# A state-space mixer on one core: half of the convolved tiles transposed by VectorE and through memory instead of TensorE

## The chip, the cores and the metric

The kernel runs on one core of a Trainium2 chip. The metric is device time in microseconds (us), the median of several runs.

## The reference

Two gated layers over `x` of shape (2, 512, 512), all in float32. Layer 0 normalizes, mixes by autocorrelation and gates by a small feed-forward block. Layer 1 normalizes, runs a Mamba-like mixer and gates by a second feed-forward block. The change lies in the mixer. Cut to what matters:

```python
proj = einsum('bsd,od->bso', h, in_proj_w)             # 512 -> 8192 gate | 8192 hid + 1024 B + 1024 C | 128 dt
hBC  = silu(causal_conv(hBC, conv_w, conv_b))          # 4 taps along the sequence
hid  = hBC[..., :8192].reshape(b, s, 128, 64)          # 128 heads of 64
hc   = (hid * dt[..., None]) in chunks of 128 steps
M    = einsum('bcihn,bcjhn->bcijh', C, B) * L          # L: decays inside a chunk
Y_diag = einsum('bcijh,bcjhp->bcihp', M, hc)
states = einsum('bclhn,bhcl,bclhp->bchpn', B, decay_states, hc)
Y_off  = einsum('bclhn,bchpn,bhcl->bclhp', C, prev_states, exp(A_cs))
y   = Y_diag + Y_off + Dp * hid
out = einsum('bsd,od->bso', rmsnorm_by_group(y * silu(gate)), out_proj_w)
```

B and C are shared by groups of 16 heads; there are 8 groups.

## The kernel before

**Tiles.** One *tile* `s` holds 128 channels (two heads) of one batch row, channels on the partitions and the 512 sequence positions (4 chunks of 128) along the free dimension. A *unit* is one group and one batch row: 8 tiles. There are 16 units and 128 tiles. A *step* `d` (63 of them, then `tail()`) treats two tiles in each of four stages at once: it finishes products for the tiles `a` = 2d, 2d+1, prepares the next pair `n` = 2d+2, 2d+3, projects and convolves the pair after that, `h` = 2d+4, 2d+5, and squares the previous pair `p`. `t` is the place of the pair in its unit: 0, 2, 4 or 6, so a unit takes four steps.

**A tile's way.** `Values` projects a pair of tiles on TensorE (seven block products instead of eight) into PSUM (`pjh`). `first_tap` and `taps` convolve (ScalarE, then three VectorE instructions), `silu()` applies SiLU on ScalarE to all that was convolved since it was last called; the result is `hid[s]`, channels on partitions. For the products the sequence positions must lie on partitions: in the next step `transposed(s)` makes four 128x128 TensorE transposes into the PSUM tile `px`, and `values(s, px)` multiplies them on VectorE by per-position, per-head factors from `sls` into `hc` (4 chunks) and `hcd` (3 chunks). `clamp` and `decays` make the decay matrices in `css[s]` (`cs`; the exponential on ScalarE, the product with `CB` on VectorE). `begun` multiplies `hcd` with the transposed B (`Bss`) on TensorE into `pn`; `states` copies chunk 0 into `st` (ScalarE) and runs the recurrence over chunks in four VectorE instructions. `starts` multiplies the loaded `eb` by C on GpSimd (POOL). In the step after, `products(s)` multiplies `hc` with the decays and `st` with `eb` into `py`, and `finish_y` scales and adds `Dp * hid` on VectorE. `Gates` projects the gate like `Values`; `Output` (`o`) does the output projection of the previous unit, spread over its steps, adding into `acc` on VectorE (L1553) and using block sums that `o.sums(0)` and `o.sums(1)` make on POOL. `pair_sums` makes the sums `sh` and `sw` of the weights on POOL. `inner` projects and convolves B and C of the next unit at t=0 (`BT`, `CT`), and `inner_products` transposes B and multiplies B and C at t=4.

**Order.** The whole part is under a manual schedule: every engine runs its instructions in the order in which the code issues them. All loads go through one queue, SP (`nc.sync`): `load_sums` (`cs`, three buffers), `load_starts` (`eb`, two), `load_rest` (`el`), `load_gate`, `load_hid` (weights `wg`, `wh`), `load_bc`, `load_out` (`wo`, once per group, 2 MB) and `load_slice`. At a step's beginning SP waits in `load_sums` for TensorE's first products, which free a `cs` buffer. The wk pool's tag `sq` has two buffers, `hid` four, `st`, `hc`, `hcd` two each. PSUM tag `tr` has one buffer, `pj` three, `yy` two, `of` and `de` one each.

57 of the 63 steps have the interleaved order (`if gates:`); steps 0 to 3, 60 and 62 have the plain one (`else:`), in which the second tile's `px` lies in a `pj` bank. Step 0 is the first of unit 0, and `head()` prepares tiles 0 to 3.

Of the kernel before, what the change touches and what calls it, by code (L numbers as in the profile page):

```python
# [15 lines left out]
P = 128  # L16
D = 512
B = 2
S = 512
# [29 lines left out]
def fused_kernel(  # L49
# [1000 lines left out]
    with ExitStack() as sm:  # L1050
# [148 lines left out]
        def finish_y(s, py):  # L1199
# [7 lines left out]
                y, hid.pop(s), Dcol[:, ct : ct + 1], y, ALU.mult, ALU.add  # L1207
            )

        def square(s):  # L1210

            u, t = divmod(s, GT)
            if t == 0:
                sums[u] = wk.tile([P, S], F32, tag="sums", name=f"sums{u}", bufs=1)
                q = sums[u]
            else:
                q = wk.tile([P, S], F32, tag="sq", name=f"sq{s}", bufs=2)
            nc.scalar.activation(q, y_of(s), AF.Square)  # L1218

            def add():  # L1220
                if t > 0:
                    nc.gpsimd.tensor_tensor(sums[u], sums[u], q, ALU.add)  # L1222

            return add
# [5 lines left out]
                nc.tensor.transpose(px[:, c, :], hid[s][:, bass.ts(c, P)], ident)  # L1230
            return px

        def values(s, px):

            u, g, b, t, h0 = place(s)
            pxh = px.rearrange("p c (h d) -> p c h d", h=2)
            hc = wk.tile([P, NCH, P], F32, tag="hc", name=f"hc{s}")
            hcd = wk.tile([P, NCH - 1, P], F32, tag="hcd", name=f"hcd{s}")
            for dst, j, n in ((hc, 0, NCH), (hcd, 1, NCH - 1)):
                nc.vector.tensor_tensor(  # L1240
                    dst.rearrange("p c (h d) -> p c h d", h=2),
                    pxh[:, 0:n],
                    pair(sls[g][:, j, b * NCH : b * NCH + n, h0 : h0 + 2]),
                    ALU.mult,
                )
            hcs[s] = hc
            return hcd
# [31 lines left out]
            return pn  # L1279

        def states(s, pn):

            u, g, b, t, h0 = place(s)
            st = wk.tile([P, NCH - 1, P], F32, tag="st", name=f"st{s}")
            nc.scalar.copy(st[:, 0, :], pn[:, 0, :])  # L1285
            for c in range(1, NCH - 1):
                for hh in range(2):
                    cols = bass.ts(hh, HP)
                    nc.vector.scalar_tensor_tensor(  # L1289
                        st[:, c, cols],  # L1290
                        st[:, c - 1, cols],
                        sls[g][:, 2, b * NCH + c, h0 + hh : h0 + hh + 1],
                        pn[:, c, cols],
                        ALU.mult,
                        ALU.add,
                    )
            sts[s] = st

        def starts(s):

# [68 lines left out]
        class Gates:  # L1369
# [65 lines left out]

        def inner_products(u):

            pb = psum.tile([P, NCH, P], F32, tag="tr", name=f"pb{u}", bufs=1)
            for c in range(NCH):
                nc.tensor.transpose(pb[:, c, :], BTs[u][:, bass.ts(c, P)], ident)  # L1440
# [9 lines left out]
            Bss[u] = wk.tile([P, NCH, NST], F32, tag="Bs", name=f"Bs{u}", bufs=1)  # L1450
# [143 lines left out]
        def head():  # L1594
# [40 lines left out]
            conv(*first)  # L1635
            conv(*channels(3))
            silu()
            nc.scalar.activation(*held, AF.Silu)

        def plain(d):  # L1640
# [4 lines left out]
        def step(d):  # L1645
# [16 lines left out]
                load_slice(h[0] // (B * GT))  # L1662
            for s in n[1:]:
                load_sums(s)
            if b == 1 and t == 0 and 0 < g < NG:
                load_out(g)
            for s in h[:1]:
                load_sums(s)
            for s in n:
                load_starts(s)  # L1670
            if n:
                load_gate(n[0] // 2)
            if h and h[0] // 2 < tiles // 2 - 1:
                whs[h[0] // 2 + 1] = load_hid(h[0] // 2 + 1)
            if b == 0 and t == 2 and 0 <= g < NG - 1:
                wbc[g + 1] = load_bc(g + 1)
            if d == steps - 2:
# [32 lines left out]
            hids = made_ahead.pop(d, None)  # L1710
            if not gates:
                first = [channels(s) for s in h[:1]]
                pxs = [transposed(s, s % 2) for s in n]

            def root():
                if t == 2 and went:
# [27 lines left out]
            if gates:  # L1744

                def output(n=1):
                    if o:
                        o.multiply(n)
# [5 lines left out]
                late = t == 2  # L1754
                px = transposed(n[0])
                hids.multiply(1, 5)
                hcd = [values(n[0], px)]
                decays(n[0], 0)
                hids.copy(0, 0)
                hids.multiply(2, 3)  # L1760
                hids.add(0, 0)
# [2 lines left out]
                output()  # L1764
                if projected is not None:
                    b_of = inner(projected, 0)
                px = transposed(n[1])
                hids.multiply(6)
                if not late:
                    added()  # L1770
                hcd.append(values(n[1], px))
                decays(n[1], 0)
                if projected is not None:
                    conv(*b_of)
                hids.copy(0, 1)
                gates.multiply(1, 5)
                decays(n[1], 1)
                starts(n[1])
                if t == 4 and o:
                    o.sums(1)  # L1780
# [50 lines left out]
                taps(*hids.sum(1))  # L1831
                output()
                added()
                states(n[1], pn)
                if projected is not None:
                    first_tap(*c_of)
                pss = squares()
                gates.multiply(3)
                silu()
                gates.add(0, 1)  # L1840
                output(int(t < 6))
                gates.silu()
                mean(pss)
# [4 lines left out]
            else:  # L1848
# [9 lines left out]
                    starts(s)  # L1858
                for f in [square(s) for s in p]:
                    f()  # L1860
                hcd = [values(s, px) for s, px in zip(n, pxs)]
                root()
                if projected is not None:
                    conv(*inner(projected, 0))
# [189 lines left out]
```

## Time and profile before

| What | Value |
|---|---|
| Time, median of 3 runs | 2217.05 us (2216.99 to 2217.43) |
| Span of the profiled execution | 2213.2 us; its own time is not listed beside it |
| TensorE (PE) busy | 2191.3 us, 99% |
| VectorE (DVE) busy | 1513.8 us, 68% |
| ScalarE (ACT) busy | 1299.4 us, 59% |
| GpSimd (POOL) busy | 1321.7 us, 60% |
| DMA engines | 146 GB/s on average |
| A unit of four interleaved steps | 104 us (208.0 us for two) |

The part under the manual schedule's `head()` and steps takes the span from about 530 us on. A line such as `L1240` is a line of the kernel printed above. A transposed second tile stands as the second `px` group of a step (L1230). "PEld" is TensorE's weight load, which overlaps its matmuls. In the timeline a TensorE group's duration contains the pipeline's tail, so groups overlap a little; the chain of waits gives the net time of each group.

### The profile page before, as it was taken

To read this page: it belongs to the slowest core of one execution; us is meant where nothing else is said; L and a number is where in the kernel's file an instruction comes from. 1 tells how busy PE (TensorE), PEld (TensorE's weight loads), DVE (VectorE), ACT (ScalarE), POOL (GpSimd) and SP (SyncE) were. 2 spreads that over 40 slices of the span, in tenths; PEclk is the share of its full clock that TensorE was granted. 3 is DMA by queue.
4 is the path that set the end of the run, shared out by engine and by line. 5 is a ranking of instruction groups with operands and counts; after the bars stand their busy time and mean duration, and the time that the engine had idled before them with its cause. 6 is when DMAs were issued, how large, how long until landed. Compare 5 with 4: busy or idle time off the path is not lost.

```text
span 2213.2 us, 35453 instructions
## 1 busy us (share of the span) xinstructions
PE 2191.3 (99%) x12460; PEld 1712.6 (77%) x12460; DVE 1513.8 (68%) x2985; ACT 1299.4 (59%) x2864; POOL 1321.7 (60%) x1234
## 2 busy tenths in 40 slices
PE   8999999999999999999999999999999999999999
PEld 4545567765568888888888888888888888888877
DVE  5263577545777777777777677777777677777763
ACT  4131323214777667676767676767767676767671
POOL 4151523323457567776766686759576866766577
PEclk9999999999999999999999999999999999999999
DMA  4012266755544446444545454454446444544452
GB/s 174 1 58 75 80 226 221 255 195 195 176 143 129 148 140 190 133 135 124 167 133 148 152 175 128 134 162 129 134 141 187 138 145 124 167 124 133 141 187 97
DMA packets 195953, 323.51 MB, mean 146 GB/s; under 512 B 17728, under 2 KB 129984, under 8 KB 193344
## 3 DMA queue, kind: packets, MB, share of 16 engines
q1 hardware_dynamic: 189376, 300.28, 44.5%
q0 software_dynamic: 6400, 20.98, 2.5%
q8 instruction: 99, 1.62, 0.3%
q14 instruction: 78, 0.64, 0.1%
HBM read 294.45 MB, written 26.74 MB: 145 GB/s over the span
## 4 chain that ended last, share of the span: by engine, by line
PE 95%; DVE 2%; ACT 1%; DMA 1%; POOL 0%; issue 0%; SPq 0%; ACTq 0%; DVEq 0%
PE pjh L607 15%; PE of L1530 15%; PE gt L607 13%; PE py L1177 5%; PE pjbc L1139 5%; PE pf L1018 4%; PE pn L1276 4%; PE py L1186 4%; PE px L1230 3%; PE ofy L1530 2%; PE hu L361 2%; PE sh L522 2%; PE pg L607 2%; PE pu L607 2%; PE gty L607 2%; PE gt L1139 2%
## 5 line engine op out<-in xcount | busy, mean ns | idle before, releaser
L1301 POOL TENSOR_TENSOR eb<-CT,eb 128x768 f32<-128x768 f32 x128 | 230.0, 1818 | 342.9 <-DMA eb<-ea_d 287.1
L1254 ACT ACTIVATE cs<-cs,sl 128x128 f32<-128x128 f32 x1024 | 325.0, 390 | 0.6 <-DMA cs<-cs_d 0.6
L1158 DVE SCALAR_TENSOR_TENSOR hid<-pjh,cw,hid 128x511 f32<-128x511 f32 (+2 forms) x384 | 286.5, 746 | 43.1 <-ACT hid L1149 35.6
L1269 DVE TENSOR_TENSOR cs<-de,CB 128x512 f32<-128x512 f32 x256 | 175.4, 685 | 80.0 <-ACT de L1268 79.0
L1688 POOL TENSOR_TENSOR y<-y,sgt 128x512 f32<-128x512 f32 x124 | 176.1, 1440 | 11.6 <-ACT sgt L1410 9.7
L1177 PE MATMUL py<-cs,hc 128*64 128x128 f32 x2048 | 180.3, 276 | 0.0
L1222 POOL TENSOR_TENSOR sums<-sums,sq 128x512 f32<-128x512 f32 x110 | 140.1, 1273 | 61.3 <-ACT sq L1218 57.6
L1268 ACT ACTIVATE de<-cs 128x512 f32<-128x512 f32 x256 | 154.0, 602 | 28.9 <-DVE cs L1269 22.6
L1186 PE MATMUL py<-eb,st 128*64 128x128 f32 x1536 | 149.1, 273 | 0.0
L1289 DVE SCALAR_TENSOR_TENSOR st<-st,sl,pn 128x64 f32<-128x64 f32 x512 | 108.4, 275 | 59.4 <-ACT st L1285 59.4
L1553 DVE SCALAR_TENSOR_TENSOR acc<-of,rg,acc 128x256 f32<-128x256 f32 x188 | 90.2, 480 | 74.7 <-PE of L1530 74.4
L1354 ACT COPY hid<-pjh 128x256 f32<-128x256 f32 x171 | 63.6, 372 | 129.5 <-PE pjh L607 127.7
L1206 DVE SCALAR_TENSOR_TENSOR y<-hid,Dcol,y 128x512 f32<-128x512 f32 x128 | 133.8, 1045 | 4.5
L1177 PEld LDWEIGHTS py<-cs,hc 128*64 128x64 f32 x2048 | 121.5, 137 | 19.9 <-issue 18.1
L1205 DVE TENSOR_TENSOR y<-py,el 128x512 f32<-128x512 f32 x128 | 87.7, 685 | 57.1 <-PE py L1186 56.3
L1285 ACT COPY st<-pn 128x128 f32<-128x128 f32 x128 | 33.1, 264 | 153.3 <-PE pn L1276 153.3
L1530 PE MATMUL of<-wt,y 128*128 128x256 f32 x512 | 121.8, 381 | 0.0
L1139 PE MATMUL pjbc<-hT,wbc 128*128 128x512 f32 x256 | 117.4, 593 | 2.1 <-DVE BT L1158 1.3
L1530 PE MATMUL of<-wo,s 128*128 128x256 f32 x496 | 118.8, 382 | 0.0
L1276 PEld LDWEIGHTS pn<-hcd,Bs 128*128 128x128 f32 x768 | 104.7, 191 | 16.5 <-issue 11.3
L607 PE MATMUL pjh<-th,sh 128*128 128x256 f32 x456 | 117.3, 380 | 0.2 <-POOL sh L581 0.2
L607 PE MATMUL pjh<-hT,wh 128*128 128x256 f32 x456 | 117.2, 379 | 0.0
(356 smaller groups left out, 5518.7 us busy)
## 6 DMA issues: line engine op xcount, KB each, us to landing
cs<-cs_d SPq DMA_DIRECT2D x128, 512.0 KB, 4.3
eb<-ea_d SPq DMA_DIRECT2D x256, 192.0 KB, 6.0
wh<-in_in_wT SPq DMA_DIRECT2D x64, 512.0 KB, 9.2
wg<-in_in_wT SPq DMA_DIRECT2D x64, 512.0 KB, 7.4
el<-ea_d SPq DMA_DIRECT2D x256, 128.0 KB, 7.5
wo<-wo_d SPq DMA_DIRECT2D x16, 1024.0 KB, 8.4
wop<-in_out_wT SPq DMA_DIRECT2D x39, 256.0 KB, 2.8
wo_d<-wop POOLq DMA_DIRECT2D x39, 256.0 KB, 2.8
```

Of the source, the lines that this page charges most:

```text
L607: nc.tensor.matmul(ps, x[:, k, :], y[:, k, :], start=(first and k == 0), stop=(k == 1), skip_group_check=True,)
L1139: nc.tensor.matmul(ps, w_of(k), hT[:, k, bass.ts(b, S)], start=(k == 0), stop=(k == KD - 1))
L1158: nc.vector.scalar_tensor_tensor(dst[:, j:], ps[:, : S - j], cw[:, ct, KCONV - 1 - j : KCONV - j], dst[:, j:], ALU.mult, ALU.add,)
L1177: nc.tensor.matmul(py[bass.ts(hh, HP), bass.ts(c, P)], hc[:, c, bass.ts(hh, HP)], M[:, hh, bass.ts(c, P)], start=True, stop=(c == 0),)
L1186: nc.tensor.matmul(py[bass.ts(hh, HP), bass.ts(c, P)], st[:, c - 1, bass.ts(hh, HP)], cte[:, hh, bass.ts(c - 1, P)], start=False, stop=True,)
L1254: nc.scalar.activation(m[:, bass.ts(c, P)], m[:, bass.ts(c, P)], AF.Relu, bias=sls[g][:, 3, b * NCH + c, h0 + hh : h0 + hh + 1], scale=-1.0,)
L1268: nc.scalar.activation(pe, m, AF.Exp, scale=-1.0)
L1269: nc.vector.tensor_tensor(m, pe, CBs[s // GT].rearrange("p c i -> p (c i)"), ALU.mult)
L1276: nc.tensor.matmul(pn[:, c, :], Bss[s // GT][:, c, :], hcd[:, c, :], start=True, stop=True)
L1301: nc.gpsimd.tensor_tensor(eb_t[s], CTs[s // GT][:, P:].unsqueeze(1).to_broadcast([P, 2, S - P]), eb_t[s], ALU.mult,)
L1530: nc.tensor.matmul(ps, x[:, k, :], y[:, k, :], start=(first and k == 0), stop=(k == 3), skip_group_check=True,)
L1688: nc.gpsimd.tensor_tensor(y_of(s), y_of(s), sgs.pop(s), ALU.mult)
```

## The change

Of each pair of tiles only the first is still transposed by TensorE. The second is taken by a new function `turn(s)`, called behind `silu()` in the step that convolves it (and in `head()` for tile 3): one VectorE transpose, which turns 32x32 blocks, into a tile `to` of tag `sq`, and four DMAs on SP that write it to a scratch tensor in memory so that rows become sequence positions, in runs of 128 elements. `fetch(s)`, at the next step's beginning on SP, reads it back (256 KB) into `to`. `values(s)` without `px` then reads it from SBUF in four instructions instead of two from PSUM.

In the interleaved steps the order moves too: the first tile's first decay comes before its values; the second tile's values come behind its second decay; `states` of the second tile is split, so that ScalarE's copy stays where it was and the four VectorE instructions come behind the turn and `gates.add(0, 1)`. In `step`'s loads, `fetch` stands behind the first `load_sums`, `load_starts` moves behind the two weight loads, and `load_out` moves to the end. In the plain steps the second tile's values follow the first's. Last, `inner_products` transposes three chunks of B instead of four (the fourth was never read), and `Bss` holds three.

```diff
+        raw, sent = {}, {}
+
+        def turn(s):
+            to = wk.tile([P, S], F32, tag="sq", name=f"tn{s}", bufs=2)
+            nc.vector.transpose(
+                to.rearrange("p (q c e) -> p q c e", q=4, c=NCH),
+                hid[s].rearrange("p (c q e) -> p q c e", c=NCH, q=4),
+            )
+            dst = dram.tile([P, 4, P], F32, tag="tn_d", name=f"tn_d{s}", bufs=3)
+            for a in range(4):
+                nc.sync.dma_start(
+                    dst[:, a, :].rearrange("(q r) e -> r q e", q=4),
+                    to[32 * a : 32 * a + 32].rearrange("r (q e) -> r q e", q=4),
+                )
+            sent[s] = to, dst
+
+        def fetch(s):
+            to, src = sent.pop(s)
+            nc.sync.dma_start(to, src.rearrange("p a e -> p (a e)"))
+            raw[s] = to.rearrange("p (a c e) -> p a c e", a=4, c=NCH)
...
-        def values(s, px):
+        def values(s, px=None):
...
             for dst, j, n in ((hc, 0, NCH), (hcd, 1, NCH - 1)):
+                if px is None:
+                    dst = dst.rearrange("p c (a e) -> p a c e", a=4)
+                    for h in range(2):
+                        two = slice(2 * h, 2 * h + 2)
+                        f = sls[g][:, j, b * NCH : b * NCH + n, h0 + h]
+                        f = f.unsqueeze(1).unsqueeze(3).to_broadcast([P, 2, n, 32])
+                        nc.vector.tensor_tensor(dst[:, two], raw[s][:, two, 0:n], f, ALU.mult)
+                    continue
...
         def states(s, pn):
+            first_state(s, pn)
+            rest_of_states(s, pn)
...
-            pb = psum.tile([P, NCH, P], F32, tag="tr", name=f"pb{u}", bufs=1)
-            for c in range(NCH):
+            pb = psum.tile([P, NCH - 1, P], F32, tag="tr", name=f"pb{u}", bufs=1)
+            for c in range(NCH - 1):
...
             silu()
+            turn(3)
...
             for s in n[1:]:
                 load_sums(s)
-            if b == 1 and t == 0 and 0 < g < NG:
-                load_out(g)
+                fetch(s)
             for s in h[:1]:
                 load_sums(s)
-            for s in n:
-                load_starts(s)
             if n:
                 load_gate(n[0] // 2)
             if h and h[0] // 2 < tiles // 2 - 1:
                 whs[h[0] // 2 + 1] = load_hid(h[0] // 2 + 1)
+            for s in n:
+                load_starts(s)
+            if b == 1 and t == 0 and 0 < g < NG:
+                load_out(g)
...
-                pxs = [transposed(s, s % 2) for s in n]
+                pxs = [transposed(s) for s in n[:1]]
...
+                decays(n[0], 0)
                 hcd = [values(n[0], px)]
-                decays(n[0], 0)
...
-                px = transposed(n[1])
                 hids.multiply(6)
...
-                hcd.append(values(n[1], px))
                 decays(n[1], 0)
...
                 decays(n[1], 1)
+                hcd.append(values(n[1]))
                 starts(n[1])
...
-                states(n[1], pn)
+                first_state(n[1], pn)
...
                 silu()
+                for s in h[1:]:
+                    turn(s)
                 gates.add(0, 1)
+                rest_of_states(n[1], pn)
...
-                hcd = [values(s, px) for s, px in zip(n, pxs)]
+                hcd = [values(*x) for x in zip(n, pxs)]
+                hcd += [values(s) for s in n[1:]]
...
                 silu()
+                for s in h[1:]:
+                    turn(s)
```

More of the change, by code (lines that the diff above doesn't have):

```diff
@@ L1231, in transposed @@
             return px
-        def values(s, px):
+        def values(s, px=None):
             u, g, b, t, h0 = place(s)
-            pxh = px.rearrange("p c (h d) -> p c h d", h=2)
+            if px is not None:
+                pxh = px.rearrange("p c (h d) -> p c h d", h=2)
             hc = wk.tile([P, NCH, P], F32, tag="hc", name=f"hc{s}")
@@ L1281, in states, with first_state, rest_of_states @@
         def states(s, pn):
+            first_state(s, pn)
+            rest_of_states(s, pn)
+        def first_state(s, pn):
+            sts[s] = wk.tile([P, NCH - 1, P], F32, tag="st", name=f"st{s}")
+            nc.scalar.copy(sts[s][:, 0, :], pn[:, 0, :])
+        def rest_of_states(s, pn):
             u, g, b, t, h0 = place(s)
-            st = wk.tile([P, NCH - 1, P], F32, tag="st", name=f"st{s}")
-            nc.scalar.copy(st[:, 0, :], pn[:, 0, :])
+            st = sts[s]
             for c in range(1, NCH - 1):
@@ L1296, in states @@
                     )
-            sts[s] = st
         def starts(s):
@@ L1449, in inner_products @@
                 )
-            Bss[u] = wk.tile([P, NCH, NST], F32, tag="Bs", name=f"Bs{u}", bufs=1)
+            Bss[u] = wk.tile([P, NCH - 1, NST], F32, tag="Bs", name=f"Bs{u}", bufs=1)
             nc.scalar.copy(Bss[u], pb)
```

## The prediction

> **What bounds the kernel now.** I read the page first: busy time and the chain that ended last.
>
> ```profile
> PE 2191.3 (99%) x12460; PEld 1712.6 (77%) x12460; DVE 1513.8 (68%) x2985; ACT 1299.4 (59%) x2864; POOL 1321.7 (60%) x1234
> PE 95%; DVE 2%; ACT 1%; DMA 1%; POOL 0%; issue 0%; SPq 0%; ACTq 0%; DVEq 0%
> ```
>
> TensorE is the bound: 95% of the chain runs over it. The waits between 640 and 2100 us hold no PE wait at all, and of PE's weight loads only `PEld of L1530 <- DVE acc L1553`, 14 times at most 0.3 us: once per unit VectorE is just late there. So time falls only by what leaves PE, less any new PE wait. The chain's order shows the price of what leaves (start, us, what):
>
> ```profile
> 1340.36 0.44 PE pb L1440 x4
> 1344.89 0.59 PE px L1230 x4
> 1350.67 0.44 PE px L1230 x4
> ```
>
> The third row is the second tile's transposes, wedged between other products: 0.435 us, 0.109 each. A unit (four steps) takes 104 us. Next, the border between a unit's first step (t=0) and its second (t=2), because VectorE and ScalarE are densest there (start, us, engine, line, form):
>
> ```profile
> 1388.23 0.83 PE L1276 MATMUL pn<-hcd,Bs 128*128 128x128 f32 x6
> 1393.85 0.39 PE L1177 MATMUL py<-cs,hc 128*64 128x128 f32 x4
> 1394.07 0.39 PE L1186 MATMUL py<-eb,st 128*64 128x128 f32 x4
> 1389.10 0.27 ACT L1285 COPY st<-pn 128x128 f32<-128x128 f32 x1 [2.01 <-PE pn L1276]
> 1389.26 0.78 ACT L1149 ACTIVATE CT<-pjbc,cb,cw 128x512 f32<-128x512 f32 x1
> 1390.06 1.28 ACT L1591 ACT_TABLE_LOAD   x1
> 1391.36 0.63 ACT L1591 ACTIVATE BT<-BT 128x512 f32<-128x512 f32 x1
> 1391.89 1.14 ACT L1591 ACTIVATE hid<-hid 128x512 f32<-128x512 f32 x2
> 1390.34 0.85 DVE L1289 SCALAR_TENSOR_TENSOR st<-st,sl,pn 128x64 f32<-128x64 f32 x4
> ```
>
> Before, the four `st` updates ran at 1390.34, during ScalarE's silus, 2.9 us before PE read the second state (1394.07). ScalarE's last silu ended at 1393.03.
>
> **Removed.** Steps 0 to 62 each lose four transposes, and 16 units one B transpose. Step 0 waits for VectorE anyway (PE idle 1.12 us before `pn` at 570.93), so 62 x 0.435 + 16 x 0.109 = 27.0 + 1.7 = **28.7 us** leave PE. The Bs copy shrinks from 0.59 us by a quarter on ScalarE, off the path.
>
> **VectorE, `values`.** Two instructions reading PSUM (0.683 and 0.547, pitches 0.60 and 0.46) become four reading SBUF. The 256-element row of L891, both inputs in SBUF, has 416 ns at least; with pitch about 0.33 for 256 and an estimated 0.265 for 192 elements, four make 1.2 us against 1.06. With POOL beside them they stretch:
>
> ```profile
> L1206 DVE SCALAR_TENSOR_TENSOR y<-hid,Dcol,y x128: 750/1043/1756, 559.1 to 2176.2; 128x512 f32<-128x512 f32 x128
> ```
>
> This instruction has two SBUF tensors; 750 ns is where POOL rests, 1043 is the median beside L1688. By 1043/750, `values` costs 1.65 contended; the top, 1756/750, would be 2.8. [...]
>
> In t=4 and t=6 steps I place them so: de-multiply done at 1326.75 (step at 1314; `hids.multiply(6)`, the copy and the clamp all come 0.44 earlier), values to 1327.95, or 1328.4 contended; the next VectorE work, `st` of the first tile, can't start before 1328.36 (ScalarE's copy, also 0.44 earlier). Covered: cost 0. If they took 2.8 us, 1.2 would show.
>
> **VectorE, the turn.** No row shows a transpose. Nearest: one-input SBUF 128x512 (L838) 480 ns; PSUM 128x512 683 ns with pitch 0.60. I take 0.62, between 0.45 and 1.5 (twice the PSUM row). [...]
>
> The turn waits for the second silu. Queued behind it on VectorE: `gates.add(0,1)` and the second tile's `st` updates, which PE reads in the next step. In t=2, 4 and 6 the cover holds. For t=6: silu ends 1365.2, turn 1365.8, add 1366.2, second state 1366.7; PE reads it at 1366.26 - 0.44 + 2.46 = 1368.3. 1.6 us are to spare.
>
> **At t=0 it does not hold.** PE comes 0.44 earlier, and so does ScalarE's row of work behind `pn`: silus end 1392.59. Turn 1392.65 to 1393.27, add to 1393.6, then 0.46 for the first two `st` updates: 1394.1. PE wants that state at 1394.07 - 0.44 = 1393.63. New wait: about 0.5, with the weight load **0.55 us**. VectorE then goes on late with the CT taps (2.25 us; they began at 1392.13, now at 1394.6) and both `y`. The hid copy on ScalarE waits for the first `y` (hid has four buffers). VectorE drops one pair of values (1.06 us) and has 3.4 us of idle time there (0.39, 1.42, 1.61), yet the step's `st` comes at 1407.6 instead of 1406.94. So `acc` is 0.66 late while PE is 0.55 - 0.44 = 0.11 late: the wait on L1553 grows by **0.55**. Fourteen units have this border: 14 x 1.1 = **15.4 us**.
>
> **SP and the DMA engines.** Five more issues per step at 0.4 to 0.5 us. The four writes stand behind the turn; queued behind them is the next step's `cs`, which waited for PE's first products anyway (L1114, 1059.6 us in all). The fetch then waits for the writes to land: the 256 KB write `wo_d<-wop` took 2.8 us, so about 1.3 us beyond `cs`. Its data land about 6 us after that `cs` was issued (512 KB `cs` rows land in 4.3), 5 us ahead of the values. [...] `eb` now stands behind the fetch, `cs`, `wg` and `wh`. The stretches show a saturated DMA (share 0.9 to 1.1) from 1320 to 1328, about 245 GB/s up to `eb` and 350 behind it. Bytes up to the last `eb`: 1.8 MB at 245 = 7.4 us, 1.0 MB at 350 = 2.9, the fetch 1.0, waiting 1.3: `eb` is ready 12.6 us after the step's first `cs` issue, against 8.6 now. POOL waits 4 us longer in most steps; it had 287 us of such waits. The next reader is `o.sums(1)` at t=4: its second sum is needed by PE at 1338.0, and POOL makes it 6.1 us after it starts on `eb`, so `eb` may be as late as 1331.9, 16.3 us after the issue at 1315.56. Cover 3.7 us; cost 0. `load_out` now last: `el` lands some 2 us before its reader; free.
>
> **Head and plain steps.** In step 0 VectorE and SP both stand behind the new turn of tile 3 (silu ended 559.2): `cs` goes from 556.7 to about 562, `eb` to about 576 for a reader at 578. With the plain steps' slightly longer values I put **2 us**, between 0 and 5.
>
> **Sum.** The profiled span is 2213.2; its own time is not listed, and 3.85 us lie between that and the median of 2217.05, kept as they are. 2213.2 - 28.7 + 15.4 + 2 = 2201.9, plus 3.85: **2205.7**; I say 2205.
>
> **Rivals.** *Full gain (0.22).* If the turn takes 0.45 and ScalarE frees it sooner, or the CT work leaves VectorE room, the border costs nothing: 2217 - 28.7 + 2 = 2190. For it: steps t=2, 4, 6 have over 1 us to spare. Against: ScalarE ran without a gap from 1389.10 to 1397.6.
>
> *Gain eaten (0.14).* A turn of 1.1 us adds 0.48 to the border twice: 14 x 0.96 = 13.4, so 2219; at 0.9, 2213. Both ends lie about the old time. For it: no row shows that operation. Against: both one-input and PSUM rows are below 0.7.
>
> *Slower (0.16): `eb` comes too late.* If small 512-byte writes or the broadcast loads pull the DMA rate down, POOL starts late, and PE stands at t=4 for `s2`. It begins 16.3 us after the step's first `cs`; with 15.4 + 2 already lost, 0.8 us past that (15 x 0.8 = 12) returns the whole gain. At 18.5: 15 x 2.2 = 33 more, 2238. For it: the DMA was already saturated and gets 0.5 MB more per step. Against: engines rest half of each step (share 0.49 over a unit).
>
> *That it doesn't do what it says* I rule out: the changed program's PE order holds one `px` group per step and three B transposes.
>
> **Numbers.** Forecast 0.48, the others 0.22, 0.14, 0.16. From no change this kernel can be told by about 0.2%, 4.4 us. Faster: 0.48 + 0.22 = 0.70; within: 0.13 of the eaten case; slower: 0.17. The range runs from full gain without a head cost (2188.4) to the upper end of the eaten case, 2220; only the late `eb` and a sliver are left out. The faster cases' own range is 2188 to 2212.
>
> **What would show it.** Right: PE's rows back to back with no second `px`; a PE or PEld wait on `st` of about 0.5 us in units 1 to 14 at t=2, and the wait on `acc` grown to 0.8. The transpose row at about 0.7 us. Values near 1.2 us at t=4, longer at t=0 and t=2. POOL's wait on `eb` up by about 150 us and more without PE waiting. Wrong: a transpose row over 1 us, PE waiting for `s` or `sh` from POOL, values waiting for the fetch, or a unit shorter by over 1.5 us (then the border was covered) or not shorter at all. A unit should fall from 104 to about 103.25 us.

## The result, and the profile after

The changed kernel is slower: 2357.94 us median (2344.19 to 2368.46, 6 runs) against 2217.02 us (2213.33 to 2217.45, 6 runs), a ratio of 1.0638, 95% interval 1.0617 to 1.0659. Forecast were 2205 us and at most 2220. The profiled execution took 2367.71 us, its span 2365.9 us. All line numbers below are those of the kernel whose profile is read; in the changed kernel the second tile's `values` are L1268 (L1270 is the PSUM form), the turn is L1214, `starts` L1337, `acc` L1589.

Busy time and the chain that ended last, on the page of the changed kernel:

```profile
PE 2223.2 (94%) x12192; PEld 1710.0 (72%) x12192; DVE 1730.5 (73%) x3174; ACT 1295.8 (55%) x2864; POOL 1337.9 (57%) x1234
PE 52%; DVE 19%; ACT 9%; DMA 8%; POOL 6%; issue 4%; SPq 2%; POOLq 0%; DVEq 0%; ACTq 0%
```

TensorE has 268 matmuls fewer and is yet busy 32 us longer; VectorE is busy 217 us longer. The chain, which ran over TensorE for 95%, now leaves it for almost half of the time. Between 640 and 2100 us no matmul had waited before. Now (who waited for whom: us in total, times, longest):

```profile
PE of L1566 <- DVE acc L1589: 47.5, 27, 4.6
PE gt L607 <- ACT sgt L1435: 21.7, 15, 2.0
PE gt L607 <- DVE sgt L1439: 10.5, 13, 0.8
```

TensorE waits for VectorE, directly or through ScalarE. What made VectorE late is seen at the turned tile (duration in ns: min/median/max):

```profile
L1268 DVE TENSOR_TENSOR hc<-tn,sl x126: 411/418/2581, 572.3 to 2306.7; 128x256 f32<-128x256 f32 x126
L1268 DVE TENSOR_TENSOR hcd<-tn,sl x126: 344/1412/2491, 573.0 to 2310.0; 128x192 f32<-128x192 f32 x126
L1214 DVE STREAM_TRANSPOSE tn<-hid x63: 700/711/715, 559.9 to 2292.5; 128x512 f32<-128x512 f32 x63
```

The transpose is steady. Most multiplications have one of two durations: 0.35 to 0.42 us (139 of 252), or 1.4 us and more (106). Two places of the timeline show when (start, us, engine, line):

```profile
1430.63 0.75 DVE L1268 TENSOR_TENSOR hc<-tn,sl 128x256 f32<-128x256 f32 x2
1431.14 3.80 POOL L1337 TENSOR_TENSOR eb<-CT,eb 128x768 f32<-128x768 f32 x2 [6.13 <-DMA eb<-ea_d]
1431.30 3.85 DVE L1268 TENSOR_TENSOR hcd<-tn,sl 128x192 f32<-128x192 f32 x2
...
1488.62 0.75 DVE L1268 TENSOR_TENSOR hc<-tn,sl 128x256 f32<-128x256 f32 x2
1489.29 0.62 DVE L1268 TENSOR_TENSOR hcd<-tn,sl 128x192 f32<-128x192 f32 x2
1491.65 3.59 POOL L1337 TENSOR_TENSOR eb<-CT,eb 128x768 f32<-128x768 f32 x2 [5.46 <-DMA eb<-ea_d]
```

The same two instructions took 0.62 us with POOL at rest (1489.29) and 3.85 us beside two POOL multiplications of together 3.80 us (1431.30): each lasted until POOL's running instruction ended. Over the trace, 144 of the 252 overlapped a POOL instruction by more than 50 ns. The 113 that took over 0.6 us all began while a POOL instruction was running, and all ended 0.21 to 0.29 us after its end. Those that began before POOL's instruction kept their 0.35 to 0.42 us; then POOL's `eb` multiplication was the one to wait, up to 2.08 us for 1.81. With the means of 939 ns (`hc`) and 1086 ns (`hcd`) in the groups, and 418 and 351 ns alone, that is 126 x 0.521 + 126 x 0.735 = 158 us of VectorE's time.

A second loss rides on the first. Four stretches of 3.41 us of the changed kernel (us, then busy time of PE, PEld, DVE, ACT and POOL, the granted TensorE clock, DMA share and rate):

```profile
1432.07:1435.49 3.42, 3.29 (x16) 2.55 (x14) 3.42 (x5) 0.91 (x3) 3.42 (x3) 1.00 0.11 31
1435.49:1438.90 3.41, 1.23 (x5) 0.81 (x6) 2.86 (x9) 2.35 (x5) 3.25 (x4) 1.00 0.00 0
1438.90:1442.31 3.41, 3.41 (x9) 2.66 (x10) 1.88 (x4) 0.00 (x0) 1.59 (x3) 0.50 0.00 0
1442.31:1445.72 3.41, 3.41 (x20) 3.10 (x19) 2.64 (x4) 2.54 (x4) 0.00 (x0) 1.00 0.00 0
```

After a stretch in which TensorE worked for 1.23 of 3.41 us, it got half its clock for the next. Over the span the mean clock is 0.981 against 1.000 before: 0.019 x 2365.9 = 45 us. That is the most that the clock can have cost. Experiment 10 below has the same matmuls and keeps TensorE busy for 2164.7 us, 58 us less than the change; the clock can explain at most 45 of these 58 us, and what the rest is was not traced.

### The profile page after: what moved, and what is told of

It reads as the page before. It is cut to its first block, busy times and chain, and to the rows that moved or that the text cites. A ratio compares the mean times of both kernels' runs of the same rounds, so it can differ in the third digit from the quotient of the medians.

```text
span 2365.9 us, 35765 instructions
## 1 busy us (share of the span) xinstructions
PE 2223.2 (94%) x12192; PEld 1710.0 (72%) x12192; DVE 1730.5 (73%) x3174; ACT 1295.8 (55%) x2864; POOL 1337.9 (57%) x1234
## 4 chain that ended last, share of the span: by engine, by line
PE 52%; DVE 19%; ACT 9%; DMA 8%; POOL 6%; issue 4%; SPq 2%; POOLq 0%; DVEq 0%; ACTq 0%
PE of L1566 9%; DMA eb<-ea_d 6%; PE pjh L607 6%; PE pf L1018 4%; DVE hcd L1268 4%; PE gt L607 4%; DVE hc L1268 3%; PE py L1177 3%; POOL eb L1337 3%; PE hu L361 2%; PE sh L522 2%; PE pg L607 2%; PE pu L607 2%; PE py L1186 2%; ACT cs L1284 2%
## 5 line engine op out<-in xcount | busy, mean ns | idle before, releaser
L1337 POOL TENSOR_TENSOR eb<-CT,eb 128x768 f32<-128x768 f32 x128 | 239.0, 1883 | 489.1 <-DMA eb<-ea_d 433.6
L607 PE MATMUL gt<-th,wg 128*128 128x256 f32 x456 | 122.9, 393 | 43.2 <-ACT sgt L1435 24.5
L1206 DVE SCALAR_TENSOR_TENSOR y<-hid,Dcol,y 128x512 f32<-128x512 f32 x128 | 147.2, 1150 | 4.5
L1566 PE MATMUL of<-wo,s 128*128 128x256 f32 x496 | 128.1, 404 | 16.2 <-DVE acc L1589 16.2
L1149 ACT ACTIVATE hid<-pjh,cb,cw 128x512 f32<-128x512 f32 x128 | 93.3, 775 | 84.4 <-DVE pjh L1395 78.0
L1306 PEld LDWEIGHTS pn<-hcd,Bs 128*128 128x128 f32 x768 | 113.3, 205 | 35.7 <-issue 16.6
L1589 DVE SCALAR_TENSOR_TENSOR acc<-of,rg,acc 128x256 f32<-128x256 f32 x188 | 90.1, 480 | 65.2 <-PE of L1566 64.9
L607 PEld LDWEIGHTS gt<-th,wg 128*128 128x128 f32 x456 | 82.6, 195 | 68.8 <-issue 45.8
L1268 DVE TENSOR_TENSOR hcd<-tn,sl 128x192 f32<-128x192 f32 x126 | 131.9, 1086 | 0.0
L1306 PE MATMUL pn<-hcd,Bs 128*128 128x128 f32 x768 | 114.3, 288 | 17.2 <-DVE hcd L1268 14.3
L1390 ACT COPY hid<-pjh 128x256 f32<-128x256 f32 x171 | 63.5, 371 | 117.1 <-PE pjh L607 102.3
L1566 PEld LDWEIGHTS of<-wo,s 128*128 128x128 f32 x496 | 97.3, 201 | 38.8 <-DVE acc L1589 24.6
```

Source lines behind the costliest of these rows:

```text
L607: nc.tensor.matmul(ps, x[:, k, :], y[:, k, :], start=(first and k == 0), stop=(k == 1), skip_group_check=True,)
L1268: nc.vector.tensor_tensor(dst[:, two], raw[s][:, two, 0:n], f, ALU.mult)
L1306: nc.tensor.matmul(pn[:, c, :], Bss[s // GT][:, c, :], hcd[:, c, :], start=True, stop=True)
L1337: nc.gpsimd.tensor_tensor(eb_t[s], CTs[s // GT][:, P:].unsqueeze(1).to_broadcast([P, 2, S - P]), eb_t[s], ALU.mult,)
L1566: nc.tensor.matmul(ps, x[:, k, :], y[:, k, :], start=(first and k == 0), stop=(k == 3), skip_group_check=True,)
```

## The experiments

The first theory was A, a collision of `values` with POOL's `starts`, brought about by the later `eb`. Its rivals were B, the trip through memory and the late loads, and C, VectorE's added work. Each ratio is to runs of the kernel before made beside the experiment; their medians were 2217.0 to 2218.1 us throughout. Experiments 3, 4, 6 to 10, 15, 16 and 18 leave out work that the result needs, and serve to time what is left.

**1. `eb` early again.**

```diff
+            for s in n:
+                load_starts(s)
             if n:
                 load_gate(n[0] // 2)
             if h and h[0] // 2 < tiles // 2 - 1:
                 whs[h[0] // 2 + 1] = load_hid(h[0] // 2 + 1)
-            for s in n:
-                load_starts(s)
```

> The changed kernel with one edit: the loads of the two `eb` tiles go back to their old place in SP's queue, ahead of `wg` and `wh` (the fetch stays ahead of them). Theory A (collision: the second tile's `values`, two SBUF inputs, run beside POOL's `starts` and are stretched from 0.3 - 0.4 us to 1.5 - 2.5 us each, because `eb` now lands just then): `eb` lands about 4 us earlier, POOL has made both `starts` before `values` begin at t=4 and t=6, the four `values` cost 1.2 - 1.7 us, and the time comes to 2195 - 2225 us. Theory B (the trip through memory: SP's queue waits for the turn, the writes and the fetch, and all later loads are late): `wg` and `wh` are late in place of `eb`; over 2300. Theory C (VectorE simply has too much work with the turn, PE waits for it): no change, 2340 - 2370.

Measured: 2377.28 us (ratio 1.0719, 1.0692 to 1.0745). Theory A in its first form fell: the place of `eb` is not what counts. The tile's rows show why:

```profile
L1268 DVE TENSOR_TENSOR hc<-tn,sl x126: 410/1242/2084, 572.0 to 2322.7; 128x256 f32<-128x256 f32 x126
L1268 DVE TENSOR_TENSOR hcd<-tn,sl x126: 343/350/2499, 574.7 to 2324.4; 128x192 f32<-128x192 f32 x126
```

Now `hc` is stretched more often than `hcd`: beyond their times alone, `hc` and `hcd` took 91 and 73 us, in the change 66 and 93. In the timeline these instructions lie beside `starts`, `sums`, `o.sums` and other POOL work: POOL is busy for more than half of the time (57% in the change), and moving one of its instructions puts another there.

**2. The order of loads alone**, in the kernel before (the opposite edit in its loads).

> The kernel before (second tile by PE, values from PSUM) with the changed kernel's order of loads alone: `wg`, `wh`, then `eb`, and `load_out` last; no turn, no fetch. A: `starts` now run beside the second tile's `values`, but these have one SBUF tensor only (the other is in PSUM), so they hardly stretch: 2212 - 2235. B: what counts is that `eb` is late; without the fetch it is late by about 3 us in place of 4 and the time goes over 2260. C: 2217, no difference.

2217.78 us (1.0002, 0.9992 to 1.0012). `values` from PSUM cost nothing beside POOL (692 ns at most, 120 of the 256 overlapping POOL work), and the later `eb` by itself costs this kernel nothing.

**3. Without POOL's `starts`.**

```diff
         def starts(s):
-            nc.gpsimd.tensor_tensor(eb_t[s], CTs[...], eb_t[s], ALU.mult)
+            pass
```

> The changed kernel with POOL's multiplication of `eb` by C left out (`starts` does nothing, PE reads `eb` as loaded); all loads, the turn, the trip through memory and the `values` stay. A: the `values` stand alone, 1.2 us for four, VectorE is on time: 2185 - 2215. B: SP's queue and the loads are as late as before; POOL being free helps little: over 2300. C: 2340 - 2370.

2255.57 us (1.0169, 1.0154 to 1.0184), between the ranges of A and B. With one of POOL's jobs gone, 102 us come back; 43 `values` instructions still overlapped other POOL work, most of them at 1.4 to 2.6 us.

**4. Without the trip through memory.**

```diff
         def turn(s):
...
-            for a in range(4):
-                nc.sync.dma_start(dst[:, a, :]..., to[32 * a : 32 * a + 32]...)
-            sent[s] = to, dst
+            sent[s] = to, None
...
-            nc.sync.dma_start(to, src.rearrange("p a e -> p (a e)"))
```

> The changed kernel without the trip through memory: the four writes and the fetch are left out, and `values` read the turned tile itself (so its blocks stay unmoved); order of loads, turn and `values` from SBUF stay. A: `eb` still stands behind `wg` and `wh` and lands only some 2 us earlier, so that `starts` still meet the `values` in part of the steps: 2230 - 2340. B: the cause is gone: 2195 - 2215. C: 2340 - 2370.

2429.57 us (1.0942, 1.0875 to 1.101). Theory B predicted about 2205 and is out: without the trip the kernel got slower, and ended above A's range as well. 193 of the 252 instructions now overlapped POOL by more than 50 ns.

**5. The `values` on POOL.** Theory A2: any POOL instruction stretches any of these four.

```diff
-                        nc.vector.tensor_tensor(dst[:, two], raw[s][:, two, 0:n], f, ALU.mult)
+                        nc.gpsimd.tensor_tensor(dst[:, two], raw[s][:, two, 0:n], f, ALU.mult)
...
+                hcd1 = values(n[1])
                 starts(n[0])
```

> The changed kernel with the second tile's `values` made by POOL in place of VectorE, ahead of `starts` in POOL's order. The first runs showed that the place of `eb` is not what counts (2377 with `eb` early, 2218 with the old kernel and `eb` late). Theory A2 (each of the four SBUF `values` on VectorE waits for whatever POOL instruction runs then, `starts`, `sums`, `o.sums`, and lasts as long as it: in the changed kernel 134 of 252 beside POOL took 158 us more than alone): on POOL they can't collide; they cost POOL about 2.6 us per step by the 730 ns of its 128x256 row, where it waits 3.8 us per `eb` now; 2185 - 2215. Theory B (late loads, the trip): the fetch and `eb` are as late as before, over 2300. Theory D (POOL becomes too slow: `starts` and `sums` come 2.6 us later): 2230 - 2300.

(The 134 in it counts overlaps of more than 150 ns.) 2271.87 us (1.0247, 1.0234 to 1.026): 86 us less than the change, but above A2's range and within D's. TensorE's wait for POOL (total, times, longest):

```profile
PE pn L1306 <- POOL hcd L1268: 43.6, 12, 7.8
```

Six of the twelve, 4 to 8 us each, lie in the six plain steps, where POOL's `values` come behind `starts` and so behind the late `eb`. Five of the regular units took 103.6 us, from `pb` to `pb` in the timeline (104.1 before).

**6. `values` from the convolved tile itself**, without turn, writes and fetch.

```diff
         def turn(s):
+            pass
         def fetch(s):
+            raw[s] = hid[s].rearrange("p (a c e) -> p a c e", a=4, c=NCH)
```

> The changed kernel without the turn, the four writes and the fetch: the second tile's `values` on VectorE read the convolved tile in SBUF itself, untransposed, in the same four instructions. What stays of the change: no second group of transposes on PE, `values` from two SBUF tensors, the order of loads. A2: the stretch stays, 2330 - 2450 (2430 was measured with the turn and without the trip). B: the trip is gone, 2190. C (VectorE's work: the turn): 44 us of it are gone, 2190 - 2260.

2434.84 to 2488.06 us in four runs (ratio 1.1057, 1.0998 to 1.1116, by the two shortest), the slowest of all, with neither turn nor trip. B and C can't explain it; what is left of the change is `values` from SBUF.

**7. One SBUF tensor in place of two.**

```diff
-                        nc.vector.tensor_tensor(dst[:, two], raw[s][:, two, 0:n], f, ALU.mult)
+                        nc.vector.tensor_scalar(dst[:, two], raw[s][:, two, 0:n], 1.0, None, ALU.mult)
```

> The changed kernel with the second tile's four `values` reading one SBUF tensor in place of two: a multiplication of the fetched tile by the constant 1.0 (so its factors are left out). Turn, writes, fetch, loads and the number and size of VectorE's instructions stay. A2: no `values` instruction is stretched beside POOL, as no one-tensor row of VectorE is in the kernel before (L1269: 691 ns at rest, 682 beside POOL): 2190 - 2215; with the border at t=0 as predicted 2205, with it covered 2190. B and C: 2330 - 2370.

2309.24 us (1.0405, 1.0391 to 1.0419). A miss for A2 as worded. The rows:

```profile
L1266 DVE TENSOR_SCALAR hc<-tn x126: 279/285/2450, 572.3 to 2264.6; 128x256 f32<-128x256 f32 x126
L1266 DVE TENSOR_SCALAR hcd<-tn x126: 246/253/2402, 572.7 to 2267.7; 128x192 f32<-128x192 f32 x126
```

One tensor, and stretched to 2.4 us all the same. The kernel before had such a row too, outside the mixer, which A2 had overlooked; its seven long cases among 64 (with `wop_more`; 548 to 965 ns) all began beside running POOL work:

```profile
L838 DVE TENSOR_SCALAR wop<-wop,gn x39: 459/480/946, 281.1 to 498.2; 128x512 f32<-128x512 f32 x39
```

In experiment 7, alone, 64 more elements cost 32 ns, two elements per ns, where the two-tensor form takes about 67 ns for them. This faster form waits for POOL too, and 2309 lies below what B and C said.

**8. The same on the convolved tile**, without turn and trip.

> As the run with values from the convolved tile in SBUF (no turn, no writes, no fetch), and these four `values` a multiplication by the constant 1.0 (factors left out): of the change only what it takes from PE is left. A2: 2186 - 2194, that is 2217.8 less the 28.7 us that were counted to leave PE; the difference to the run with one tensor and the turn is what turn, trip and border cost (15 us as predicted, 0 if covered). B: the same. C: 2186 - 2194 and the run with the turn far above.

2358.42 us (1.0616, 1.0575 to 1.0656): the same miss.

**9. Transposes in the place of the multiplications.** Theory A3: a lock that only some forms of instruction take. (Its "two elements per cycle" is a guess; measured are the 32 ns for 64 elements of experiment 7.)

```diff
-                        nc.vector.tensor_tensor(dst[:, two], raw[s][:, two, 0:n], f, ALU.mult)
+                        nc.vector.transpose(dst[:, two], raw[s][:, two, 0:n])
```

> The changed kernel with the second tile's four `values` replaced by four VectorE transposes of the same blocks of the fetched tile (32x32 blocks turned in place of the multiplication: factors left out, elements turned); turn, trip, loads, number of instructions stay. Multiplying by a constant did not help (2309): that form, 283 ns alone for 256 elements, was stretched to 1.3 - 1.9 us beside POOL as well, while the 63 turns (SBUF to SBUF too, 700 to 715 ns) never were. Theory A3 (a lock: a VectorE instruction that reads two SBUF tensors, or one at two elements per cycle, waits until POOL's running instruction ends; others do not): no stretch at all, about 0.4 us each, PE waits for `acc` gone, regular units 103.2 - 103.7 us, 2200 - 2216. Theory A2b (any VectorE instruction from SBUF to SBUF at this place is stretched): 2300 or more. Theory C (VectorE has too much work): 2300 or more.

2229.02 us (1.0046, 1.0034 to 1.0058): **129 of the 141 us are gone**, with turn, trip, loads, number and places of VectorE's instructions as in the change. It is still 13 us above A3's range.

```profile
L1266 DVE STREAM_TRANSPOSE hc<-tn x126: 400/420/436, 571.4 to 2167.8; 128x256 f32<-128x256 f32 x126
L1266 DVE STREAM_TRANSPOSE hcd<-tn x126: 333/335/340, 572.1 to 2168.4; 128x192 f32<-128x192 f32 x126
```

Alone these cost what the multiplications cost alone (418 and 351), and the longest is 436 ns, though 159 of the 252 overlapped POOL. The clock is back at 0.996; its share of the 129 is at most 45 - 0.004 x 2229.3 = 36 us.

**10. The same without turn and trip** (experiment 6 with these transposes).

> The same (four transposes in place of the multiplications), reading the convolved tile itself, without the turn, the four writes and the fetch. A3: nothing but what PE loses is left, 2186 - 2196; its distance to the run with turn and trip is what the turn and the trip cost (15 + 2 us as predicted). A2b and C: 2300 or more.

2193.62 us (0.9894, 0.988 to 0.9908): 24.4 us less than the 2218.06 of the kernel before beside it. This is the worth of TensorE's part, less a wait that came with it: without any turn, weight loads wait longer for `acc` (the kernel before, then experiment 10; total, times, longest):

```profile
PEld of L1530 <- DVE acc L1553: 4.0, 15, 0.3
PEld of L1551 <- DVE acc L1574: 8.4, 15, 0.8
```

Turn and trip cost the other 35.4.

**11 and 12. POOL's `values` where they pay.**

```diff
+        def by_turn(s):
+            d = (s - 3) // 2
+            t = 2 * d % GT
+            return 0 < d < steps - 1 and not plain(d) and t != 2
```

(Tiles for which this is false keep TensorE's transposes and `values` from PSUM; experiment 12 leaves out `and t != 2`.)

> A version meant to be faster than both: the second tile's `values` by POOL, ahead of `starts`, as in the run that took 2272, but only where it pays: in the short-handed steps at both ends (where POOL's `values` stood behind late `starts` and PE waited 4 - 8 us for them, seven times), and in the steps with t=2 (whose turn falls into the t=0 border), TensorE transposes the tile as before and VectorE makes the values from PSUM. A3 with the border as predicted: 3 x 0.435 + 0.109 less per regular unit, 104.1 to 102.7 - 103.0 us, 2195 - 2207. If the trip through memory or POOL's 2.3 us per step cost something of their own: 2210 - 2230.

> The same with the steps t=2 by POOL as well (TensorE only at both ends). A3: the border at t=0 is back, regular units 103.6 us as the even ones of the run with all `values` on POOL, 2205 - 2216; the distance to the run without t=2 is the border (predicted 1.1 us less 0.435, in 14 units: 9 us). If the border costs nothing: 0.435 less per unit than the run without t=2, some 6 us faster than it.

2206.95 us (0.995, 0.9938 to 0.9962), and 2225.64 us (1.0035, 1.0022 to 1.0047), above its range. ("Seven times" should read six, as in experiment 5.) The first beats both kernels, at the upper end of what was expected; its units took 102.8 to 104.8 us. The distance of 19 us is twice what the border was thought to cost, so something else stood in the turn's way. The timeline of experiment 9, at the end of a step with t=4:

```profile
931.03 0.71 DVE L1214 STREAM_TRANSPOSE tn<-hid 128x512 f32<-128x512 f32 x1 [1.51 <-POOL sums L1243]
931.66 0.38 DVE L1437 TENSOR_TENSOR sgt<-sgt,gt 128x256 f32<-128x256 f32 x1
931.97 0.84 DVE L1324 SCALAR_TENSOR_TENSOR st<-st,sl,pn 128x64 f32<-128x64 f32 x4
932.96 0.52 PE L1474 MATMUL pb<-ident,BT 128*128 128x128 f32 x3 [1.37 <-DVE st L1324]
```

The turned tile lies in the `sq` ring, whose buffer POOL's addition to `sums` must free first (1.51 us in the first row); POOL is late there, behind `starts` and `o.sums(1)`. The `st` updates stand behind the turn, and `pb` needs the one `tr` bank that they read `pn` from (1.37 us in the last row).

**13 to 16. The turn behind the `st` updates**, in experiments 12, 11 and 9; and 9 without the trip.

```diff
-                for s in h[1:]:
-                    turn(s)
                 gates.add(0, 1)
                 rest_of_states(n[1], pn)
+                for s in h[1:]:
+                    turn(s)
```

> `values` by POOL in all regular steps (the run that took 2225.6), and the turn moved behind the second tile's `st` updates on VectorE, that is after `gates.add(0, 1)` and `rest_of_states`. T1 (the turn stands ahead of the four `st` updates, and these hold up PE twice: the state itself at t=0, and at t=4 the one PSUM bank that `pn` and `pb` share, freed only by the last `st`; waits of 0.4 to 2 us on `pb` per unit): these waits go, 2206 - 2217. T2 (the trip: SP's queue and the loads behind the writes and the fetch): no change or slower, since the writes start 1 us later, 2224 - 2235.

> The same with TensorE's transposes in the steps t=2 (the run that took 2207), turn behind the `st` updates. T1: the waits on `pb` (up to 1.8 us in every second unit) go, 2196 - 2204. T2: 2205 - 2212.

> The run with four transposes in place of the multiplications (2229; factors left out, elements turned), with the turn behind the `st` updates. T1: 2210 - 2221. T2: 2226 - 2236.

> The run with four transposes in place of the multiplications (2229), with the turn as in the change, but without the four writes and the fetch (the transposes read the turned tile itself). T1: the turn is nearly all of the 35 us between it and the run with neither (2193.6), 2222 - 2231. T2: the trip is most of it, 2196 - 2212. In parts: 2212 - 2222.

- 13: 2230.31 us (1.0059, 1.0038 to 1.0081), no gain, a miss for T1; the number lies in T2's range, but the waits are others. Its units alternate between 102.8 and up to 109.6 us. In every second one, at t=2, POOL makes the sums of the output weights and `o.sums(0)` ahead of the `values`, and TensorE now waits there (total, times, longest), 2.6 to 3.7 us each time:

```profile
PE pn L1315 <- POOL hcd L1277: 19.6, 6, 3.7
```

In experiment 12, with the same order on POOL, these waits were 0.6 us (2.5 in all). Why they grew by more than the turn's move gave back is not shown.

- 14: 2205.19 us (0.9956, 0.9942 to 0.997), not told apart from experiment 11, a little above T1's range and at the lower edge of T2's.
- 15: 2216.27 us (0.9999, 0.9988 to 1.0011), 12.8 us less than experiment 9, as T1 said; the waits on `pb` are gone between 640 and 2100 us.
- 16: 2228.44 us (1.0055, 1.0042 to 1.0068), against 2229.02 with the trip. **Four writes and a fetch per step cost nothing that can be told here**: both intervals are about 3 us to either side.

**17 and 18. `eb` early again**, in experiments 14 and 15 (the edit of experiment 1).

> The fastest version so far (2205.2: `values` by POOL in regular steps except t=2, turn behind the `st` updates) with the `eb` loads back ahead of `wg` and `wh`. What PE still waits for there in some units is POOL's `sh` (0.7 to 1.9 us per unit in five units, units of 103.3 - 104.4 us instead of 102.7). T3 (POOL is late since it stands waiting for `eb`): these waits go, 2198 - 2203. T4 (POOL has too much to do, wherever `eb` stands): 2203 - 2210.

> The run with four transposes in place of the multiplications and the turn behind the `st` updates (2216.3; factors left out, elements turned), with the `eb` loads back ahead of `wg` and `wh`. This asks what the late `eb` costs by itself once nothing waits on the lock: T3: its waits for POOL's `sh` (0.4 - 2.5 us in six units, 5.9 us in the second) go, 2204 - 2212. T4: 2213 - 2220. Then the 12 us and more that are left over the run without turn and trip are VectorE's own (`acc` 0.76 per unit, first and last units).

17: 2207.76 us (0.9962, 0.9949 to 0.9974), no gain: T4 for that version. 18: 2208.93 us (0.9969, 0.9957 to 0.998), 7.3 us less than experiment 15: T3. One edit, made in experiment 1, cost 19 us there, where POOL's work met other `values` (164 us lost to it in place of 158, and a granted clock of 0.975 in place of 0.981), and brings 7 here, where no `values` wait for POOL.

## Why the prediction was wrong

The path from the kernel before to the change, as steps between measured medians (us):

| Step | us | predicted |
|---|---|---|
| TensorE's transposes gone, `acc` waits come (10 against before) | -24.4 | -28.7 |
| turn and trip, placed so that neither `st` nor `eb` suffers (18 against 10) | +15.3 | +17.4, with the fourth row |
| `eb` behind the weights (15 against 18) | +7.3 | 0 |
| turn ahead of the `st` updates (9 against 15) | +12.8 | in the second row |
| the `values` waiting for POOL (change against 9) | +128.9 | 0 |
| sum | +139.9 | -11.3 |

The rows depend on this order of steps. The second is the least pure: experiment 10 still has `eb` behind the weights, experiment 18 doesn't.

**The step that failed is "VectorE, `values`".** It had the right row before it: 750 ns where POOL rests, 1043 and 1756 beside it. It read them as a ratio and scaled four short instructions by it, to 1.65 us or at most 2.8, and put their cost at 0. Measured, the four durations add up to 2 x (0.939 + 1.086) = 4.05 us on average. At rest four took 1.29 us (1488.62 to 1489.91), near the 1.2. The excess is not in proportion to the instruction. It is the rest of POOL's instruction, 1.1 to 1.8 us mostly, the same for a VectorE instruction of 0.35 us, and there were four in a row where before there had been none: 113 stretched instructions, each 1.40 us above its time alone, make the 158 us. These two numbers are from the trace after. The trace of before could have shown the kind of cost, for the row from which the prediction took its 416 ns was itself stretched beside POOL, six times of 33 and up to 1521 ns:

```profile
L891 DVE TENSOR_TENSOR it<-it,uq x33: 416/420/1521, 281.5 to 512.4; 128x256 f32<-128x256 f32 x33
```

A ratio of 1043/750 or 1756/750 doesn't give that; a wait does. The row that tells the kinds apart was in the trace of before as well:

```profile
L1269 DVE TENSOR_TENSOR cs<-de,CB x256: 672/683/693, 546.4 to 2154.2; 128x512 f32<-128x512 f32 x128
```

One input in PSUM, 256 times, 161 of them overlapping POOL work: never over 693 ns. Moving an input from PSUM to SBUF is what the change does to `values`, and this row beside L1206 and L891 says what that does.

The runs tell the forms apart: two SBUF inputs took 3.85 us beside POOL's 3.80 (two `hcd` instructions of the change), experiment 7's `tensor_scalar` with one SBUF input up to 2450 ns (285 in the median), while the row with one input in PSUM stayed at 693 at most and experiment 9's transposes at 436. The prediction had no term for such a wait.

**"Covered: cost 0"** failed with it, and one thing was not laid together: the step on SP and the DMA engines put `eb` 4 us later, at 1315.56 + 12.6 = 1328.2, right where the `values` were to end (1327.95, or 1328.4 contended), and didn't ask what POOL would be running beside them. Experiment 1 shows that this alone would not have saved the sum.

**Removed**: right in kind. The units fell from 104.1 to 102.3 and 102.8 us in turn, where 4 x 0.435 + 0.109 says 102.25 (experiment 10). In nine of its units, among them those of 102.8, weight loads wait 0.6 to 0.8 us for `acc`, in the others 0.3 as before.

**The turn**: 0.62 us were taken, as a distance to the next instruction; its duration is 0.711 and that distance 0.635, so this term was right. The border at t=0 came out near its number: in experiment 9, weight loads wait for the state and for `acc` (total, times, longest)

```profile
PEld of L1564 <- DVE acc L1587: 10.7, 14, 0.8
```

0.8 us in 14 units; and 0.4 us in 14 for `st` (0.8 and 0.55 were forecast). The wait for `st` is the turn's: it is gone in experiments 10 and 15. Most of the wait for `acc` is not, and here the number was right by luck: without any turn it is 8.1 us in the same 14 units, against 3.7 in the kernel before (experiment 10, 640 to 2100 us), and what makes it was not traced. **"In t=2, 4 and 6 the cover holds" failed at t=4.** The step asked who reads the second state, not who waits for the bank that the `st` updates read, nor what the turn's own buffer waits for. With TensorE's waits of experiment 9

```profile
PE pb L1474 <- DVE st L1324: 5.6, 7, 1.4
PE pjh L607 <- ACT hid L1388: 4.7, 6, 1.2
```

most of the 12.8 us are accounted for: in experiment 15 no matmul waits for `st` any more between 640 and 2100 us, and the second wait is 1.3 us in all, 9 us less together.

**SP and the DMA engines**: the cost 0 of the trip was right (experiment 16; in the change a write landed in 1.8 us and the fetch in 4.1, medians), and TensorE hardly waited for `s2` (3.8 us for `s` in the change). The late `eb` cost 7.3 us by other readers: matmuls waited 9.3 us for POOL's `sh` in experiment 15 and 3.7 in 18, and the turn waited 4.7 us for POOL's `sums`, whose `sq` buffers it needs, and then not at all. The rival "`eb` comes too late" had the sign and not the mechanism.

**Head and plain steps**: 2 us were put there, 0 to 5. In experiment 18 the units of the plain steps and the end took 4.5, 2.0 and 2.0 us more than in experiment 10: 8.5.

**What would show it**: "Wrong: ... values waiting" named the fetch; they waited for POOL. "POOL's wait on `eb` up by about 150 us" came true (287.1 to 433.6), and so did the sign of being wrong that units would not get shorter: from 640 us on they took 106.8 to 121.3 us.

## What to carry to other kernels

Before an operand moves from PSUM to SBUF, look for a VectorE row with two SBUF inputs in the trace and compare its minimum with its maximum: in this case the difference is an amount of time, the rest of whatever POOL is running (416 to 1521 ns in L891, 344 to 2581 in the `hcd` and `hc` rows of the change), and it is paid once per instruction, so four short instructions can pay it four times (4.05 us on average in place of 1.29). Where such work must be in SBUF, it can go to POOL itself in front of its other work, but only in steps where POOL has the room (experiments 11 and 14: 0.995 and 0.9956; in all steps, experiment 5: 1.0247); or one input stays in PSUM (L1269: 693 ns at most). For a new instruction in a full queue ask three things: who reads what stands behind it, whose buffer that work frees, and whose buffer it needs itself.

## What the runs showed of the hardware

- VectorE's transpose from SBUF to SBUF never waited for POOL: 699 to 715 ns in 63 turns, 61 of them beside POOL, and 333 to 340 ns for the 128x192 form, 89 of 126 beside POOL (experiment 9). Alone it costs about what a multiplication of the same size costs (420 and 335 ns against 418 and 351).
- POOL made the same four multiplications at steady speed (experiment 14; ns: min/median/max):

```profile
L1277 POOL TENSOR_TENSOR hc<-tn,sl x84: 618/628/642, 646.5 to 2067.6; 128x256 f32<-128x256 f32 x84
L1277 POOL TENSOR_TENSOR hcd<-tn,sl x84: 505/517/530, 647.6 to 2068.7; 128x192 f32<-128x192 f32 x84
```

- In the changed kernel the granted clock fell to a half 19 times before the end of the span, in stretches of 3.4 us or multiples of it, 92 us in all. Each followed a stretch of 3.4 us in which TensorE had been idle for 1.9 us or more. Six times this idle time lay in two gaps, each of 0.9 to 2.0 us (1.39 the longer one in the case shown); six times it lay in one gap of 1.9 to 2.8 us; in the other seven the gap was 3.4 to 5.6 us. The 1.9 us is no fixed threshold: near its end experiment 9 got half its clock after stretches with 1.13 and 1.20 us idle.
